# Three more ring slots and one more row group ahead in the second half of a sparse attention

## The chip, the cores and the metric

The kernel runs on one core of one Trainium2 chip. The metric is the device time of one execution in microseconds (us). Before the change the median of three runs was 1874.77 us (1874.08 to 1879.82).

A core has engines that run their own instruction streams side by side: TensorE (PE in the profile; PEld is its weight load), VectorE (DVE), ScalarE (ACT), GpSimd (POOL) and SyncE (SP), and 16 DMA engines that move data. An engine works its stream in order and waits on semaphores for the others.

## The reference

One layer of graph attention over 4096 nodes with 512 features and 8 heads, followed by a feed-forward part. The adjacency matrix is 4096 x 4096 and sparse: the mean row has some 17 ones.

```python
hs = layer_norm(x, ln1_scale, ln1_bias)
ht = layer_norm(h_target, ln1_scale, ln1_bias)
q = (ht @ Wq + bq).reshape(T, H, HD) / sqrt(HD)
k = (hs @ Wk + bk).reshape(S, H, HD)
v = (hs @ Wv + bv).reshape(S, H, HD)
logits = where(adj != 0, einsum('thd,shd->hts', q, k), -1e30)
ctx = einsum('hts,shd->thd', softmax(logits), v).reshape(T, D)
ht = layer_norm(ht + ctx @ Wo + bo, ln2_scale, ln2_bias)
out = layernorm(x + ht + gelu(ht @ W1) @ W2)
```

(The masks of the nodes are left out here; all nodes are valid.)

## The kernel before

Keys and values of all nodes are computed once and stored in HBM as rows of 1024 numbers (`kvd`: 512 of key, 512 of value). From the adjacency matrix the kernel makes, per target node, the list of its neighbours. The targets are sorted by their degree and cut into 32 tiles of 128 targets; a tile has a cap, the largest number of neighbours that it provides for. This is done in two parts, the first and the second 2048 targets, so that the attention on the first part can run while the lists of the second are still made.

The attention then works in row groups. A group is up to three neighbours of each of a tile's 128 targets: three gathers of GpSimd, each of which fetches 128 rows of `kvd` into one slot of a ring in SBUF. There are 603 gathers in 211 groups; groups 106 to 210 belong to the second part.

```python
NA, NBT = len(CAPS_A), len(CAPS_B)
S = 3
RING = 17
...
ring = kp.tile([P, RING, 2 * D], F32, name="kv")     # 17 slots of 128 x 1024 numbers
...
SG = [(i, j0, min(S, cap - j0)) for i, (_, cap) in enumerate(TILES)
      for j0 in range(0, cap, S)]
place = [0]
for _, _, n in SG:
    if place[-1] + n > RING:
        place[-1] = 0
    place.append(place[-1] + n)
...
def issue(k):
    if k >= len(SG):
        return
    i, j0, n = SG[k]
    if j0 == 0:
        prefetch(i + 2)                    # the list of a later tile
        if i not in tqs:
            fronts[i] = front(i)           # the query tile: gather, norm, projection
            step(fronts, i)
        ...
    kvs[k] = ring[:, place[k]:place[k] + n, :]
    for j in range(n):
        gather(kvs[k][:, j, :], kvd[0:N + 1, :], recs[i][:, E0 + j0 + j:E0 + j0 + j + 1])
```

A group's work: VectorE multiplies the key halves with the query (line 1169) and sums per head (line 1173), ScalarE takes the exponential (lines 1177 and 1187), VectorE weights two of the three value halves (line 1132), ScalarE the third, eight heads one by one (line 1152). In the second part VectorE adds two of them (line 1136). TensorE then transposes and adds up the value halves in PSUM (`cps`, line 1140). The weighting of a group comes after the product of the next one:

```python
for k in range(AHEAD + 1):                       # AHEAD = 4
    issue(k)
...
    kv, tq = kvs.pop(k), tqs[i]
    nc.vector.tensor_tensor(kv[:, :n, :D], kv[:, :n, :D], ..., ALU.mult)      # line 1169
    nc.vector.tensor_reduce(lg[:, :n, :], ..., AX.X, ALU.add)                 # line 1173
    ...
    if pend:
        values(*pend.pop())          # the group before: lines 1132, 1136, 1140
        issue(k + AHEAD)             # rows of the group four further on
    ...
```

At the end of a tile `finish` divides by the sums, projects and normalises (lines 1037 to 1097). Beside the attention runs a second stream, `feed`: the feed-forward part of the tiles that are done (lines 1277 and 1286 on TensorE), with a gather of x and a store of the result on GpSimd (lines 952 and 1254). All gathers and stores stand in the one queue of GpSimd, as do small power operations for the norms (line 674).

The lists have work space of their own: two buffers of 4 KB per partition (`a`), three of 1 KB (`sg`) and small ones (`dec`, `dif`, `rank`, `ranki`, `b16`). They are last used when the lists of the second part are sorted and written out.

```python
a = lp.tile([P, QW], I32, name="a", bufs=2)
sg = lp.tile([P, QW], U8, name="sg", bufs=3)
dec = lp.tile([P, 2, SEG, 8], U16, name="dec")
```

Of the kernel before, what the change touches and what calls it, by code (L numbers as in the profile page):

```python
# [8 lines left out]
F32 = mybir.dt.float32  # L9
I32 = mybir.dt.int32  # L10
U8 = mybir.dt.uint8
# [6 lines left out]
P = 128  # L18
# [348 lines left out]
BF16 = mybir.dt.bfloat16  # L367
U8 = mybir.dt.uint8
U16 = mybir.dt.uint16
# [74 lines left out]
def adj_resnorm_kernel(  # L444
# [34 lines left out]
    N, D = x.shape  # L479
# [9 lines left out]
    QW = N // NQ  # L489
# [4 lines left out]
    SEG = NQ * SQ  # L494
# [6 lines left out]
    NA, NBT = len(CAPS_A), len(CAPS_B)  # L501
    PARTS = ((0, len(CAPS_A)), (len(CAPS_A), len(CAPS_B)))
    S = 3
    RING = 17

    const = ctx.enter_context(tc.tile_pool(name="const", bufs=1))
    dram = ctx.enter_context(tc.tile_pool(name="dram", bufs=1, space=DRAM))
# [22 lines left out]
    with tc.tile_pool(name="keep", bufs=1) as keep:  # L530
# [17 lines left out]
        with ExitStack() as late:  # L548
            lp = late.enter_context(tc.tile_pool(name="lists", bufs=1))
            kp = late.enter_context(tc.tile_pool(name="kv", bufs=1))  # L550
# [9 lines left out]

            ring = kp.tile([P, RING, 2 * D], F32, name="kv")

            def xrows(n):
                return ring[:, 12 + n % 5, :].rearrange("p (j d) -> p j d", j=G)
# [27 lines left out]
            one_c = lp.tile([P, 1], F32, name="one_c")  # L594

            def list_constants():
                io = lp.tile([P, QW], I32, name="a", bufs=2)
                nc.gpsimd.iota(io[:, :SQ * WS], pattern=[[0, SQ], [2, WS]], base=1,
                               channel_multiplier=0)

                nc.vector.tensor_copy(lio, io[:, :WQ])
                io = lp.tile([P, QW], I32, name="a", bufs=2)
                nc.gpsimd.iota(io[:, :2 * SEG], pattern=[[1, 2], [QW, NQ], [2 * WS, SQ]], base=0,
                               channel_multiplier=0)
                nc.gpsimd.iota(io[:, 2 * SEG:2 * SEG + NB], pattern=[[1, NB]], base=0,
                               channel_multiplier=0)

                nc.vector.tensor_copy(segoff.rearrange("p b q s -> p (b q s)"), io[:, :2 * SEG])
                nc.vector.tensor_copy(bins, io[:, 2 * SEG:2 * SEG + NB])

                nc.gpsimd.memset(lower, -1.0)
                nc.gpsimd.affine_select(out=lower, in_=lower, compare_op=ALU.is_ge, fill=0.0,
                                        base=0, pattern=[[-1, P]], channel_multiplier=1)
                for R, (i0, n) in zip(Rs, PARTS):
# [80 lines left out]
            def quarter(i, h):  # L695
                if i < NA + FILL:
                    a = ring[:, (i * NQ + h) % DEEP, :].bitcast(I32)
                else:
                    a = lp.tile([P, QW], I32, name="a", bufs=2)
                nc.sync.dma_start(a, adj[i * P:(i + 1) * P, h * QW:(h + 1) * QW])  # L700
                return a

            def edges(i):

                part = 1 if i >= NA else 0
                rec = Rs[part][:, i - PARTS[part][0], :]
                cand = lp.tile([P, SEG, 8], U16, name="cand", bufs=2)
                for h in range(NQ):
                    n = i * NQ + h
                    while len(adjs) < min(n + 2, NT * NQ):  # L710
                        adjs.append(quarter(*divmod(len(adjs), NQ)))
                    a, adjs[n] = adjs[n], None

                    sg = lp.tile([P, QW], U8, name="sg", bufs=3)
                    nc.scalar.activation(sg, a, AF.Sign, accum_out=dpart[:, i, h:h + 1])  # L715
                    ahead = min(n + DEEP - 1, n + 3 + n // 2)
                    while len(adjs) < min(max(n + 3, min(ahead, (NA + FILL) * NQ)), NT * NQ):
                        adjs.append(quarter(*divmod(len(adjs), NQ)))
                    wd = sg.bitcast(U16)
                    nc.vector.tensor_tensor(wd, wd, lio, ALU.mult)  # L720
                    for s, (w0, w1) in enumerate(SEGS):
                        nc.vector.max(cand[:, h * SQ + s, :], wd[:, w0:w1])  # L722
                    if h == 1:
                        keep_rest()
                    if h % 2 and moms:
                        moments(moms.pop(0))
                    yield 2.0
                dec = lp.tile([P, 2, SEG, 8], U16, name="dec")
                nc.vector.tensor_single_scalar(dec[:, 0], cand, 255, op=ALU.bitwise_and)
                nc.vector.tensor_single_scalar(dec[:, 1], cand, 8, op=ALU.logical_shift_right)  # L730
                gid = lp.tile([P, 2 * SEG, 8], F32, name="gid")
                dec = dec.rearrange("p b s e -> p (b s) e")
                off = segoff.rearrange("p b q s -> p (b q s)")
                nc.vector.scalar_tensor_tensor(gid, dec, 0.0,
                                               off.unsqueeze(2).to_broadcast([P, 2 * SEG, 8]),
                                               op0=ALU.is_gt, op1=ALU.mult)
                nc.vector.tensor_add(gid, gid, dec)
                flat = gid.rearrange("p s e -> p (s e)")
                for r in range(RE // 8):
                    top = rec[:, E0 + r * 8:E0 + (r + 1) * 8]  # L740
# [53 lines left out]
            def sort(part):  # L794

                i0, n = PARTS[part]
                me = slice(i0, i0 + n)
                pool, R = lp, Rs[part]
                nc.vector.tensor_reduce(deg[:, me], dpart[:, me, :], AX.X, ALU.add)
                nc.vector.tensor_copy(R[:, :, DEG], deg[:, me])  # L800
                dif = pool.tile([P, n], F32, name="dif")
                nc.vector.scalar_tensor_tensor(dif, deg[:, me], float(RE), cnt[:, me], op0=ALU.min,
                                               op1=ALU.not_equal)
                nc.vector.tensor_reduce(bad[:, 1 + part:2 + part], dif, AX.X, ALU.max)
                nc.vector.tensor_scalar(dif, deg[:, me], 0.0, float(NB - 1), op0=ALU.max,
                                        op1=ALU.min)
                b16 = pool.tile([P, n], BF16, name="b16")
                nc.vector.tensor_scalar(b16, dif, -1.0, float(NB - 1), op0=ALU.mult, op1=ALU.add)
                if part:
                    oh = pool.tile([P, QW], I32, name="a", bufs=2).bitcast(BF16)  # L810
                else:
                    oh = wp.tile([P, NB * n], BF16, name="oh")
                oh = oh[:, :NB * n].rearrange("p (b i) -> p b i", b=NB)
                nc.vector.tensor_tensor(oh, b16.unsqueeze(1).to_broadcast([P, NB, n]),
                                        bins.unsqueeze(2).to_broadcast([P, NB, n]), ALU.is_equal)
                ohf = oh.rearrange("p b i -> p (b i)")
                pos = pool.tile([P, QW], I32, name="a", bufs=2).bitcast(F32)
                pos = pos[:, :NB * n].rearrange("p (b i) -> p b i", b=NB)
                posf = pos.rearrange("p b i -> p (b i)")
                w = NB * n // 2  # L820
# [12 lines left out]
                    nc.tensor.matmul(pa, lower, ohf[:, sl], start=True, stop=True)  # L833
                    nc.vector.tensor_add(posf[:, sl], pa, posf[:, sl])
                nc.vector.tensor_mul(pos, pos, oh)
                rank = pool.tile([P, n], F32, name="rank")
                nc.vector.tensor_reduce(rank, pos.rearrange("p b i -> p i b"), AX.X, ALU.add)
                ranki = pool.tile([P, n], I32, name="ranki")
                nc.vector.tensor_copy(ranki, rank)
                yield 10.0  # L840
                for i in range(n):
# [157 lines left out]
                  for j0 in range(0, cap, S)]  # L999
            kvs, rests, fronts = {}, {}, {}  # L1000
            place = [0]
            for _, _, n in SG:
                if place[-1] + n > RING:
                    place[-1] = 0
                place.append(place[-1] + n)

            def step(gens, i):

                if i in gens and next(gens[i], StopIteration) is StopIteration:
                    del gens[i]  # L1010

            def issue(k):

                if k >= len(SG):
                    return
                i, j0, n = SG[k]
                if j0 == 0:
                    prefetch(i + 2)
# [96 lines left out]
            def attention():  # L1115
# [35 lines left out]
                        v = kv[:, S - 1, D + hd * HD:D + (hd + 1) * HD]  # L1151
                        nc.scalar.mul(v, v, pa[:, hd:hd + 1])  # L1152

                for k in range(AHEAD + 1):
                    issue(k)
                yield 0.0
                k = 0
                for group in GROUPS:
# [3 lines left out]
                    for i in group:  # L1162
                        cps = ps.tile([P, KC, P], F32, name="cps", bufs=2)
                        while k < len(SG) and SG[k][0] == i:
                            _, j0, n = SG[k]
# [13 lines left out]
                            yield cost * n  # L1179
                            if pend:  # L1180
                                values(*pend.pop())
                                issue(k + AHEAD)
                            advance()
                            if j0 == 0:

# [165 lines left out]
            def prepare():  # L1351
# [6 lines left out]
                for R, (i0, n) in zip(Rs, PARTS):  # L1358
                    Rf = R.bitcast(F32)
                    nc.vector.tensor_copy(Rf[:, :, RST], rs[:, i0:i0 + n])  # L1360
                    nc.vector.tensor_copy(Rf[:, :, RST + 1], nm[:, i0:i0 + n])
                nm = lp.tile([P, QW], I32, name="a", bufs=2)
                nc.sync.dma_start(nm[:NT, :P], nodemask.rearrange("(c p) -> c p", p=P))
                nmf = nm.bitcast(F32)[:NT, P:2 * P]
                nc.vector.tensor_scalar(nmf, nm[:NT, :P], 1.0, None, op0=ALU.not_equal)
# [69 lines left out]
```

## Time and profile before

| | value |
|---|---|
| median time of three runs | 1874.77 us |
| span of the profiled execution | 1873.0 us |
| mean granted clock of TensorE | 0.963 |
| row gathers (line 952, `kv`) | 603, 690.1 us of GpSimd |
| idle time of GpSimd before them | 499.2 us |
| row products (line 1169) | 211, 352.5 us of VectorE |
| idle time of VectorE before them | 108.9 us, of it 97.8 us for gathers |
| transposes of values (line 1140) | 2008, 264.5 us of TensorE, idle before them 54.2 us |
| feed-forward (lines 1277 and 1286) | 3200 matmuls, 946.2 us of TensorE |

A busy share is an average over stages. A line of a group names the source line, the engine, what is written and read, how often, the busy time and the mean of one, and then how long the engine stood idle before these instructions and who released it. A line of waits has the engine and line that waited, the one waited for, the total, the number of times and the longest. A line of stretches has, for each stretch of the span, the busy time of PE, PEld, DVE, ACT and POOL, the granted clock of TensorE (1.00 is full), the busy share of the DMA engines and GB/s.

### The profile page before, as it was taken

What the parts mean: (1) busy time and instruction counts of PE and PEld (TensorE: products, weight loads), DVE (VectorE), ACT (ScalarE), POOL (GpSimd) and SP (SyncE); (2) the same over time, 40 slices, a digit from 0 to 9 for tenths busy, and PEclk for the clock granted to TensorE, in tenths of its full rate; (3) what the DMA queues carried; (4) which work ended last, traced back from release to release, by engine and by line L of the source; (5) the groups of instructions that cost most, each with busy time, mean ns of one, the idle gap of its engine ahead of it and who ended that gap; (6) DMA issues with size and microseconds to landing.
All of it is one profiled execution on the core that took longest, in us unless ns stands there. A gap on an engine that the chain in (4) does not pass through costs nothing. (4 is left out here: it accounts for less than half of the span.)

```text
span 1873.0 us, 22926 instructions
## 1 busy us (share of the span) xinstructions
PE 1699.6 (91%) x7030; PEld 1097.4 (59%) x7030; DVE 1430.0 (76%) x2595; ACT 1242.5 (66%) x3133; POOL 881.9 (47%) x804
## 2 busy tenths in 40 slices
PE   7989884698998989999999989999999999999996
PEld 3444332466655656766666656566666566666664
DVE  6999855989998838677878889889877778788400
ACT  5777634577886737776777767777777677777411
POOL 1000143744545474656666666656555545554101
PEclk9999977898999999999999989999999999999998
DMA  9999949978877556777778778767676767766000
GB/s 348 375 373 377 348 154 341 330 269 300 306 276 252 203 170 213 262 242 258 260 248 283 276 268 279 267 229 251 225 240 227 259 219 236 238 222 222 23 1 24
DMA packets 147757, 463.28 MB, mean 247 GB/s; under 512 B 24468, under 2 KB 29160, under 8 KB 147624
## 3 DMA queue, kind: packets, MB, share of 16 engines
q0 software_dynamic: 95696, 342.19, 53.9%
q1 hardware_dynamic: 44112, 96.44, 14.5%
q10 hardware_dynamic: 7816, 23.08, 3.2%
q8 instruction: 58, 0.95, 0.2%
q14 instruction: 75, 0.61, 0.1%
HBM read 430.76 MB, written 30.89 MB: 246 GB/s over the span
## 5 line engine op out<-in xcount | busy, mean ns | idle before, releaser
L952 POOL DMA_INDIRECT kv<-kvd,rec x603 | 690.1, 1144 | 499.2 <-PE cps L1140 232.9
L1277 PE MATMUL pf<-h2T,w 128*128 128x256 f32 (+1 forms) x2176 | 475.6, 371 | 1.2 <-ACT h2T L1097 1.2
L1286 PE MATMUL po<-w,gt 128*128 128x512 f32 x1024 | 470.6, 601 | 3.3 <-ACT gt L1280 3.3
L1169 DVE TENSOR_TENSOR kv<-kv,tq 128x1536 f32<-128x1536 f32 (+2 forms) x211 | 352.5, 1676 | 108.9 <-DMA kv<-kvd,rec 97.8
L1277 PEld LDWEIGHTS pf<-h2T,w 128*128 128x128 f32 x2176 | 391.6, 193 | 65.8 <-issue 19.8
L1152 ACT ACTIVATE kv<-kv,pa 128x64 f32<-128x64 f32 x1520 | 391.5, 336 | 3.6
L1173 DVE TENSOR_REDUCE lg<-kv 128x24 f32<-128x1536 f32 (+2 forms) x211 | 350.7, 1668 | 1.7 <-ACT pa L1149 0.2
L1140 PE MATMUL cps<-ident,kv 128*128 128x128 f32 x2008 | 264.5, 279 | 54.2 <-DVE kv L1132 40.3
L1140 PEld LDWEIGHTS cps<-ident,kv 128*128 128x128 f32 x2008 | 238.0, 144 | 128.9 <-issue 49.2
L1286 PEld LDWEIGHTS po<-w,gt 128*128 128x128 f32 x1024 | 188.6, 193 | 193.8 <-issue 189.4
L1132 DVE TENSOR_TENSOR kv<-kv,p 128x1024 f32<-128x1024 f32 (+1 forms) x211 | 249.5, 1189 | 53.5 <-ACT p L1177 53.5
L674 POOL TENSOR_TENSOR n_rs<-n_ve,mhalf 128x2 f32<-128x2 f32 (+2 forms) x51 | 47.1, 924 | 335.2 <-DVE n_ve L667 150.9
L1280 ACT ACT_TABLE_LOAD x110 | 141.1, 1283 | 1.7
L917 PE MATMUL pq<-wk,h2T 128*128 128x512 f32 x256 | 125.3, 634 | 15.8 <-ACT h2T L902 8.1
L722 DVE MAX8 cand<-sg 128x8 uint16<-128x103 uint16 (+1 forms) x640 | 131.9, 251 | 0.5
L991 PE MATMUL t<-wq,tq 128*128 128x512 f32 x256 | 118.5, 606 | 10.8 <-ACT tq L985 8.0
L715 ACT ACTIVATE sg<-kv 128x1024 uint8<-128x1024 int32 x84 | 88.7, 1058 | 56.8 <-DMA kv<-in_adj_dram 23.4
L1280 ACT ACTIVATE gt<-pf 128x512 f32<-128x512 f32 x128 | 76.4, 597 | 75.0 <-PE pf L1277 73.9
L1067 PE MATMUL t<-wo,rb 128*128 128x512 f32 x256 | 119.2, 610 | 3.6 <-DVE rb L1057 3.6
L917 PE MATMUL pq<-wv,h2T 128*128 128x512 f32 x256 | 116.7, 598 | 1.3 <-ACT tq L919 1.3
L917 PEld LDWEIGHTS pq<-wk,h2T 128*128 128x128 f32 x256 | 49.8, 202 | 81.9 <-issue 51.4
L1177 ACT ACT_TABLE_LOAD x67 | 86.0, 1283 | 9.2 <-DVE lg L1173 7.4
(157 smaller groups left out, 1544.4 us busy)
## 6 DMA issues: line engine op xcount, KB each, us to landing
kv<-in_adj_dram SPq DMA_DIRECT2D x84, 512.0 KB, 7.5
a<-in_adj_dram SPq DMA_DIRECT2D x44, 512.0 KB, 6.4
kvd<-tq ACTq DMA_DIRECT2D x24, 512.0 KB, 6.6
kv<-kvd,rec POOLq DMA_INDIRECT x603, 5.7
kv<-in_L_gnn_h_target_dram SPq DMA_DIRECT2D x32, 256.0 KB, 7.7
kv<-in_x_dram SPq DMA_DIRECT2D x15, 512.0 KB, 8.9
rest_d<-gid SPq DMA_DIRECT2D x32, 160.0 KB, 5.0
w<-in_L_gnn_W_dram SPq DMA_DIRECT2D x4, 1024.0 KB, 9.5
```

What stands on the lines that cost most here:

```text
L722: nc.vector.max(cand[:, h * SQ + s, :], wd[:, w0:w1])
L917: nc.tensor.matmul(pkv, hT[:, kc, j * P:(j + 1) * P], w[:, kc, :], start=kc == 0, stop=kc == KC - 1)
L952: nc.gpsimd.indirect_dma_start(out=dst, out_offset=None, in_=table[:, :], in_offset=bass.IndirectOffsetOnAxis(ap=idx, axis=0))
L1067: nc.tensor.matmul(pa, ct[:, c, :], wo[:, c, :], start=False, stop=c == KC - 1, skip_group_check=True)
L1132: nc.vector.tensor_tensor(v4, v4, p[:, j0:j0 + m, :].unsqueeze(3) .to_broadcast([P, m, H, HD]), ALU.mult)
L1140: nc.tensor.matmul(cps[:, c, :], kv[:, j, D + c * P:D + (c + 1) * P], ident, is_transpose=True, start=j0 + j == 0 and c == 0, stop=j0 + n ...
L1152: nc.scalar.mul(v, v, pa[:, hd:hd + 1])
L1169: nc.vector.tensor_tensor(kv[:, :n, :D], kv[:, :n, :D], tq[:, :D].unsqueeze(1).to_broadcast([P, n, D]), ALU.mult)
L1173: nc.vector.tensor_reduce(lg[:, :n, :], kv[:, :n, :D].rearrange("p j (h d) -> p j h d", h=H), AX.X, ALU.add)
L1277: nc.tensor.matmul(pf[:, k, :], w1[(f0 + k) // KC][:, kc, (f0 + k) % KC * P:((f0 + k) % KC + 1) * P], h2T[:, kc, :w], start=kc == 0, stop= ...
L1280: nc.scalar.activation(gt, pf, AF.Gelu_apprx_tanh)
L1286: nc.tensor.matmul(po[j], gt[:, k, j * P:(j + 1) * P], w2[(f0 + k) // KC][:, (f0 + k) % KC, :], start=False, stop=f0 + k == FC - 1, skip_g ...
```

## The change

From the second part on, the ring has 20 slots in place of 17, and the rows are requested five groups ahead in place of four. The room for the three slots comes from the lists: their work buffers are no longer allocated for themselves but lie in slots 17 to 19, which the first part of the attention doesn't use and which are free when the second part needs them. It is meant to give the row gathers of the second part more time before their rows are needed.

```diff
-    RING = 17
+    RING = (17, 20)
...
-            ring = kp.tile([P, RING, 2 * D], F32, name="kv")
+            ring = kp.tile([P, RING[1], 2 * D], F32, name="kv")
+            wide = [ring[:, 17 + i, :].bitcast(I32) for i in range(2)]
+            tools = ring[:, 19, :]
+            signs = [tools[:, i * QW // 4:(i + 1) * QW // 4].bitcast(U8) for i in range(3)]
+            dec_w = tools[:, 768:768 + SEG * 8].bitcast(U16).rearrange(...)
...
-                    a = lp.tile([P, QW], I32, name="a", bufs=2)
+                    a = turn_of("wide", wide)          # so at all six places of "a"
...
-                    sg = lp.tile([P, QW], U8, name="sg", bufs=3)
+                    sg = turn_of("signs", signs)
...
-                dif = pool.tile([P, n], F32, name="dif")
+                dif, rank = tools[:, 928:928 + n], tools[:, 944:944 + n]
+                ranki, b16 = tools[:, 960:960 + n].bitcast(I32), tools[:, 976:984].bitcast(BF16)
...
-            for _, _, n in SG:
-                if place[-1] + n > RING:
+            for i, _, n in SG:
+                if place[-1] + n > RING[i >= NA]:
                     place[-1] = 0
                 place.append(place[-1] + n)
+            first_b = next(k for k, (i, _, _) in enumerate(SG) if i >= NA)
...
+            def request(k):
+                ahead = AHEAD + (1 if k >= first_b else 0)
+                while issued[0] <= min(k + ahead, len(SG) - 1):
+                    issue(issued[0])
+                    ...
+                    issued[0] += 1
...
-                for k in range(AHEAD + 1):
-                    issue(k)
+                request(0)
...
                                 values(*pend.pop())
-                                issue(k + AHEAD)
+                                request(k)
```

More of the change, by code (lines that the diff above doesn't have):

```diff
@@ L559, in adj_resnorm_kernel, with turn_of @@
             psi = mid.enter_context(tc.tile_pool(name="psi", bufs=1, space=PSUM))
-            ring = kp.tile([P, RING, 2 * D], F32, name="kv")
+            ring = kp.tile([P, RING[1], 2 * D], F32, name="kv")
+            wide = [ring[:, 17 + i, :].bitcast(I32) for i in range(2)]
+            tools = ring[:, 19, :]
+            signs = [tools[:, i * QW // 4:(i + 1) * QW // 4].bitcast(U8) for i in range(3)]
+            dec_w = tools[:, 768:768 + SEG * 8].bitcast(U16).rearrange("p (b s e) -> p b s e",
+                                                                       b=2, s=SEG)
+            turns = {"wide": 0, "signs": 0}
+            def turn_of(name, places):
+                turns[name] += 1
+                return places[turns[name] % len(places)]
             def xrows(n):
@@ L596, in list_constants @@
             def list_constants():
-                io = lp.tile([P, QW], I32, name="a", bufs=2)
+                io = turn_of("wide", wide)
                 nc.gpsimd.iota(io[:, :SQ * WS], pattern=[[0, SQ], [2, WS]], base=1,
@@ L601, in list_constants @@
                 nc.vector.tensor_copy(lio, io[:, :WQ])
-                io = lp.tile([P, QW], I32, name="a", bufs=2)
+                io = turn_of("wide", wide)
                 nc.gpsimd.iota(io[:, :2 * SEG], pattern=[[1, 2], [QW, NQ], [2 * WS, SQ]], base=0,
@@ L727, in edges @@
                     yield 2.0
-                dec = lp.tile([P, 2, SEG, 8], U16, name="dec")
+                dec = dec_w
                 nc.vector.tensor_single_scalar(dec[:, 0], cand, 255, op=ALU.bitwise_and)
@@ L806, in sort @@
                                         op1=ALU.min)
-                b16 = pool.tile([P, n], BF16, name="b16")
                 nc.vector.tensor_scalar(b16, dif, -1.0, float(NB - 1), op0=ALU.mult, op1=ALU.add)
                 if part:
-                    oh = pool.tile([P, QW], I32, name="a", bufs=2).bitcast(BF16)
+                    oh = turn_of("wide", wide).bitcast(BF16)
                 else:
@@ L816, in sort @@
                 ohf = oh.rearrange("p b i -> p (b i)")
-                pos = pool.tile([P, QW], I32, name="a", bufs=2).bitcast(F32)
+                pos = turn_of("wide", wide).bitcast(F32)
                 pos = pos[:, :NB * n].rearrange("p (b i) -> p b i", b=NB)
@@ L835, in sort @@
                 nc.vector.tensor_mul(pos, pos, oh)
-                rank = pool.tile([P, n], F32, name="rank")
                 nc.vector.tensor_reduce(rank, pos.rearrange("p b i -> p i b"), AX.X, ALU.add)
-                ranki = pool.tile([P, n], I32, name="ranki")
                 nc.vector.tensor_copy(ranki, rank)
@@ L1001, in adj_resnorm_kernel @@
             place = [0]
-            for _, _, n in SG:
-                if place[-1] + n > RING:
+            for i, _, n in SG:
+                if place[-1] + n > RING[i >= NA]:
                     place[-1] = 0
                 place.append(place[-1] + n)
+            first_b = next(k for k, (i, _, _) in enumerate(SG) if i >= NA)
+            issued = [0]
             def step(gens, i):
@@ L1010, in step @@
                     del gens[i]
+            def request(k):
+                ahead = AHEAD + (1 if k >= first_b else 0)
+                while issued[0] <= min(k + ahead, len(SG) - 1):
+                    issue(issued[0])
+                    mine = set(range(place[issued[0]], place[issued[0]] + SG[issued[0]][2]))
+                    for m in range(k, issued[0]):
+                        assert not mine & set(range(place[m], place[m] + SG[m][2]))
+                    issued[0] += 1
             def issue(k):
-                if k >= len(SG):
-                    return
                 i, j0, n = SG[k]
@@ L1361, in prepare @@
                     nc.vector.tensor_copy(Rf[:, :, RST + 1], nm[:, i0:i0 + n])
-                nm = lp.tile([P, QW], I32, name="a", bufs=2)
+                nm = turn_of("wide", wide)
                 nc.sync.dma_start(nm[:NT, :P], nodemask.rearrange("(c p) -> c p", p=P))
```

## The prediction

> **What bounds the kernel now.** I read the page first: the busy shares, then the stretches of the second part of the attention, then the waits in it by engine, last the order of time around single waits.
>
> ```profile
> PE 1699.6 (91%) x7030; PEld 1097.4 (59%) x7030; DVE 1430.0 (76%) x2595; ACT 1242.5 (66%) x3133; POOL 881.9 (47%) x804
> ```
>
> TensorE is busy for 91% of the span, so it is the engine whose gaps are worth anything. The chain of waits of the page covers only the last 17 us and tells nothing of the part that the change touches; I left it. The change acts from group 106 of 211 on (the first row group of tile 16). In the trace its product (line 1169) starts at 1042.3 us and the last one, of group 210, at 1733.6 us. So I cut the span there, with columns of busy us per engine, the granted clock and the share of the DMA engines:
>
> ```profile
> 1040.00:1220.00 180.00, 164.09 (x701) 111.70 (x700) 157.21 (x160) 132.03 (x364) 119.46 (x102) 0.93 0.79 266
> 1220.00:1740.00 520.00, 502.67 (x2128) 334.50 (x2127) 418.37 (x446) 380.96 (x989) 283.28 (x255) 0.99 0.70 231
> 1740.00:1873.00 133.00, 114.31 (x488) 76.56 (x486) 15.83 (x77) 27.34 (x55) 11.28 (x13) 0.95 0.05 17
> ```
>
> TensorE idles 180 - 164.1 = 15.9 us in the first stretch and 520 - 502.7 = 17.3 us in the second: 33 us in all. That is the whole stock of idle time that a change to the second part can take away, 1.8% of the span. The clock tells a second, smaller stock: 0.93 in the first stretch. Now who waits for whom between 1040 and 1740 us (total, times, longest):
>
> ```profile
> POOL kv L952 <- PE cps L1140: 77.8, 52, 6.4
> POOL kv L952 <- DVE kv L1136: 76.3, 36, 5.8
> ...
> DVE kv L1169 <- DMA kv<-kvd,rec: 37.2, 20, 6.8
> ...
> PE cps L1140 <- DVE kv L1136: 13.9, 6, 5.0
> ```
>
> GpSimd stands for 154 us before row gathers, because the ring slot they write is still being read (77.8 + 76.3). VectorE stands for 37.2 us because rows have not landed. TensorE stands for only 13.9 us behind the value half of the ring (line 1136, after which the transposes of line 1140 run). This falling series, 154, 37, 14, is the point: most of the wait is slack and only its end reaches the bound. The rest of TensorE's 33 us are waits for ScalarE in the front and finish of a tile (line 982 6.0, 1063 5.1, 991 4.0, 1093 3.4 us, summed from its gaps), which no ring slot cures.
>
> How one such gap comes about, in order of time (start, length, engine, line; idle before it in brackets), GpSimd first, then VectorE, then TensorE:
>
> ```profile
> 1181.78 2.54 POOL L1254 DMA_INDIRECT out_dram<-xt,rec  x1 [0.30 <-ACT kv L1152]
> 1187.35 0.97 POOL L952 DMA_INDIRECT xt<-in_x_dram,rec  x1 [3.02 <-DMA out_dram<-xt,rec]
> ...
> 1202.37 1.76 DVE L1169 TENSOR_TENSOR kv<-kv,tq 128x1536 f32<-128x1536 f32 x1 [4.43 <-DMA kv<-kvd,rec]
> ...
> 1200.45 3.60 PE L1067 MATMUL t<-wo,rb 128*128 128x512 f32 x8
> 1207.58 1.97 PE L1140 MATMUL cps<-ident,kv 128*128 128x128 f32 x8 [3.53 <-DVE kv L1136]
> ```
>
> GpSimd is held by a store and by a gather of x, the row gathers of group 133 go out late (1189.9 to 1196.7 us), VectorE's product for them starts 4.43 us late, the weighting of the group before stands behind it on VectorE, and TensorE loses 3.53 us. The half clock follows; the same view of the four short stretches after the cps gaps:
>
> ```profile
> 1056.50:1059.90 3.40, 3.34 (x12) 3.07 (x13) 1.23 (x2) 3.40 (x13) 2.79 (x3) 0.50 0.96 284
> 1090.60:1097.40 6.80, 3.84 (x11) 2.77 (x12) 6.80 (x7) 6.53 (x18) 4.09 (x4) 0.50 0.85 282
> ...
> 1135.00:1138.40 3.40, 3.40 (x6) 1.34 (x5) 3.40 (x3) 1.67 (x2) 2.39 (x2) 0.50 0.98 236
> 1206.70:1213.50 6.80, 5.92 (x13) 3.45 (x14) 5.75 (x8) 3.74 (x15) 3.39 (x4) 0.50 0.78 249
> ```
>
> **What the Trainium skill says.** "Perfetto Trace Analysis", Optimization Strategy: a gap that keeps repeating on the engine that should be full can mean too little SBUF for the next tile. The 154 us of GpSimd agree in kind; but the gap is on GpSimd, not on the full engine, which is why I count little of it. "TensorE: Matmul & The Clock Gate", What's actually happening: the array falls to half clock after an idle window of about 3.4 us and needs about as long of work to come back. The trace agrees: stretches of 3.4 and 6.8 us at 0.50 beside gaps of 2.15 to 5.00 us. The same page, Architectural detail, says that GpSimd works its queue strictly in order; the trace agrees (1187.35 us above: the gathers wait behind the store's landing). "DMA: Bandwidth & Descriptors", Rules for kernel authors: issue a DMA early and wait for it late. A gather here takes 5.5 us from issue to landing (median, 4.1 to 7.4), and from the end of a group's last gather to its use I find 11.5 us in the median, but under 6.2 us in 11 of the 105 groups, 7 of them among the first 28. Those few are what is to be gained.
>
> **The change, part by part.**
>
> *Work.* No gather, product or matmul is added or removed: 603 gathers, 211 groups. Only where the rows lie and when they are asked for changes.
>
> *List work space in the ring.* The same number of buffers (two wide, three sign), now parts of slots 17 to 19. In the built program the order on every engine, and nearly every wait, is that of before until the end of the first part, since rows there still use 17 slots and four groups ahead. I expect nothing before some 1000 us: 0 us. The lists' last use of that space is the 16 scatters of the second part's records, the last from 676.8 us; the first row group of the second part is gathered from 1028.9 us, some 350 us later, so nobody waits for the three slots.
>
> *Three more slots.* With 17 slots, a group of the second part overwrites the slot of the group 5 or 6 before it (59 and 42 groups); with 20, of the one 6 or 7 before it (54 and 46). Each request also stands one group earlier in the program. Tied together: a gather waits for the same event as before, but is for the next group. A group lasts (1733.6 - 1042.3) / 104 = 6.6 us, so the time between landing and use grows by some 6.6 us where GpSimd is waiting for a slot. Leads of 4.4 to 6.2 become 11 to 13 us against 5.5 us of landing. The waits of VectorE for rows should fall from 37.2 us to 5 to 10.
>
> *What of this reaches TensorE.* The cps gaps, 13.9 us. Then the half clock behind them: work done at half clock takes twice its time, so half of its busy time is lost: (3.34 + 3.84 + 3.40 + 5.92) / 2 = 8.3 us. Together 22.2 us.
>
> *What I take off.* In the built program row gathers stand 3 to 5 gathers earlier against the other GpSimd instructions nearly everywhere, but around the pair of stores and x gathers near gather 380 they stand where they did. That is the gap at 1207 us, 3.5 us and 3.0 us of clock, which I leave: 15.7 us remain. Of those I count four fifths, because once VectorE has its rows it runs into other waits (28.5 us for the probabilities of ScalarE, 37.4 us for the query product): 12.6 us.
>
> *End.* After 1740 us only the feed-forward part is left, 114 us of TensorE work in 133 us. It is unchanged and starts earlier by what was saved.
>
> Sum: 1874.8 - 12.6 = 1862, which I round to 1861, as earlier requests may shave some of the front waits too.
>
> **Rivals.** (1) *Hidden anyway.* VectorE's lateness is taken up by the other stream on TensorE, and the gaps move to the ScalarE waits: saving 0 to 5 us, 1870 to 1875. For it: VectorE's two other large waits in this stretch, 28.5 and 37.4 us, have nothing to do with rows. Against: of the four largest gaps of TensorE in the second part (5.00, 3.53, 3.34, 2.86 us) three stand directly before cps. (2) *All of it.* Every row wait goes, the clock stays up and the fronts, which start a group earlier, lose their waits too: 33 us plus some 13 us of half clock (seven stretches, 26.4 us busy) give a floor of 1829. Against: fronts and finishes keep their distances in program order. (3) *A new wait.* More rows in flight fill the DMA queues (0.79 busy already in the first stretch), or GpSimd blocks in its queue for a query tile not yet free, or the scheduler's new local order hurts ScalarE: 5 to 15 us lost, 1880 to 1890. Against: bytes are the same, and the wait of query gathers for the finish (line 1063) is 0.3 us here.
>
> **Range and chances.** The middle is 1861. Below, rival 2 in half reaches 1848; above, rival 1 ends at 1875. I take 1848 to 1875. Faster by over 2% means under 1837, which needs over 37 of at most 46 us: 0.05. Slower by over 2% means over 1912; nothing in the change costs that: 0.02.
>
> **What would show it.** Right: in the first 1000 us the two profiles agree; from there the waits of VectorE for rows fall below 12 us, the wait of cps for line 1136 below 5 us, and the half-clock stretches between 1050 and 1220 us go from five to one or two. GpSimd's waits for slots stay near 150 us, as the ring is full again, one group further on. Wrong: VectorE's row waits vanish and TensorE's idle time in the second part stays near 33 us (rival 1), or gaps before lines 982, 991 and 1063 grow. A difference before 1000 us would mean that the shared work space costs waits that I did not see.

## The result, and the profile after

The changed kernel takes 1882.36 us (median of four runs, 1879.70 to 1885.35). The kernel before, run beside it, takes 1876.01 us. The ratio is 1.0032 with a 95% interval of 1.0007 to 1.0056. I had expected 1861 us, in a range of 1848 to 1875: the change costs 0.3% where I expected it to bring 0.7%.

The page of the changed kernel shows the same busy TensorE in a slightly longer span:

```profile
PE 1698.0 (90%) x7030; PEld 1097.0 (58%) x7030; DVE 1429.2 (76%) x2595; ACT 1233.1 (66%) x3127; POOL 887.3 (47%) x804
```

The second part, cut at the same times as in the prediction (busy us of PE, PEld, DVE, ACT and POOL, granted clock, share of the DMA engines, GB/s):

```profile
1040.00:1220.00 180.00, 167.68 (x731) 114.11 (x730) 163.74 (x166) 136.96 (x387) 121.44 (x106) 0.97 0.82 281
1220.00:1740.00 520.00, 488.00 (x2052) 324.83 (x2051) 408.70 (x439) 365.16 (x956) 279.46 (x246) 0.98 0.66 222
```

The two halves of the second part go opposite ways. In the first stretch TensorE idles 180 - 167.7 = 12.3 us, where it idled 15.9, and its clock is 0.97 for 0.93: a gain. In the second it idles 520 - 488 = 32.0 us, where it idled 17.3, and its clock is 0.98 for 0.99: a loss. If each matmul is set against the matmul of the same number in the trace before, the changed kernel is 7 us ahead when the second part begins (TensorE's order of instructions is the same up to there, so I take this for scatter), 16 us ahead at 1290 us and 4 us behind at the end. About 9 us were won up to 1290 us, and 20 us lost after it.

The waits of the same 700 us (engine and line that waited, released by; total, times, longest). The lines of the changed kernel are numbered some 20 higher: 1157 is the addition that was 1136, 1161 the transposes of values that were 1140, 1189 the product that was 1169; 992, 995 and 1001 are the front's transposes, its copies by ScalarE and its query matmul; 1084 and 1092 are the finish's transposes and its copy of h.

```profile
POOL kv L962 <- DVE kv L1157: 77.9, 36, 7.1
...
POOL kv L962 <- PE cps L1161: 59.1, 31, 5.9
...
DVE kv L1189 <- DMA kv<-kvd,rec: 22.3, 13, 6.3
...
PE t L1084 <- ACT tq L995: 11.1, 2, 7.3
...
PE t L992 <- ACT h L1092: 8.7, 2, 5.9
...
PE cps L1161 <- DVE kv L1157: 5.8, 2, 4.2
```

VectorE's wait for rows fell from 37.2 to 22.3 us, and TensorE's wait for the value half from 13.9 to 5.8 us. In the place of these stand two waits of TensorE for ScalarE, 11.1 and 8.7 us; the same pairs were 3.0 and 3.6 us before:

```profile
PE t L982 <- ACT h L1071: 3.6, 2, 3.3
PE t L1063 <- ACT tq L985: 3.0, 2, 1.6
```

All waits of TensorE for ScalarE in this stretch sum to 37.1 us; before, to 16.6.

How the largest gap comes about, in order of time (start, length, engine, line; idle before it in brackets):

```profile
1466.07 0.60 PE L992 MATMUL t<-ident,tq 128*128 128x128 f32 x4
...
1467.38 2.74 PE L1306 MATMUL po<-w,gt 128*128 128x512 f32 x6
...
1468.47 2.02 ACT L1173 ACTIVATE kv<-kv,pa 128x64 f32<-128x64 f32 x8
...
1470.86 1.22 DVE L1189 TENSOR_TENSOR kv<-kv,tq 128x1024 f32<-128x1024 f32 x1 [1.30 <-DMA kv<-kvd,rec]
...
1472.61 1.21 DVE L1193 TENSOR_REDUCE lg<-kv 128x16 f32<-128x1024 f32 x1
...
1473.85 0.19 ACT L1197 ACTIVATE p<-lg 128x16 f32<-128x16 f32 x1 [3.37 <-DVE lg L1193]
1474.06 1.28 ACT L1300 ACT_TABLE_LOAD   x1
1475.35 0.60 ACT L1300 ACTIVATE gt<-pf 128x512 f32<-128x512 f32 x1
1475.84 1.50 ACT L995 ACTIVATE tq<-t,b1r,cols 128x128 f32<-128x128 f32 x4
1477.39 1.12 PE L1084 MATMUL t<-ident,tq 128*128 128x128 f32 x4 [7.28 <-ACT tq L995]
```

TensorE writes the front's transposes into the PSUM tile `t` at 1466.1 us. The next user of `t` is the finish (line 1084), and it needs the front's copies (line 995) done. They are 1.5 us of work, but in ScalarE's list they stand behind a third value half of 2.02 us, an exponential that waits 3.37 us for VectorE's logits, and a GELU with its table load. They start at 1475.8 us, over 9 us after the transposes, and end at 1477.3 us, 10.7 us after them. In that time TensorE has only some 3.5 us of other work (its last, line 1306, ends at 1470.1 us), so it stands for 7.28 us.

Half clock comes with the new gaps as it came with the old ones:

```profile
1054.00:1057.40 3.40, 3.13 (x14) 3.04 (x15) 2.04 (x3) 1.77 (x8) 2.48 (x4) 0.50 0.88 298
1108.60:1115.40 6.80, 6.01 (x18) 4.90 (x19) 6.80 (x7) 4.44 (x13) 1.19 (x2) 0.50 0.76 270
...
1381.70:1388.50 6.80, 3.28 (x10) 2.84 (x11) 6.35 (x14) 5.36 (x15) 3.62 (x5) 0.50 0.41 125
1473.80:1480.60 6.80, 3.21 (x7) 1.93 (x8) 4.62 (x9) 3.46 (x7) 3.51 (x5) 0.50 0.95 353
```

The last two stretches begin 2.4 and 3.7 us after their gap began, while TensorE still stands, so half of each holds no matmul (3.28 and 3.21 us of 6.80 are busy). The four transposes at 1477.39 us take 1.12 us at half clock, those at 1466.07 us 0.60 us at full clock.

Between 1050 and 1220 us 10.2 us of half clock are left. But there are 20.4 us of it between 1290 and 1573 us, and the sum over the second part is 30.6 us in both kernels.

### The profile page after: what moved, and what is told of

The parts are those of the page before. It is cut to its first block, busy times and chain, and to the rows that moved or that the text cites. A ratio compares the mean times of both kernels' runs of the same rounds, so it can differ in the third digit from the quotient of the medians.

```text
span 1877.7 us, 22906 instructions
## 1 busy us (share of the span) xinstructions
PE 1698.0 (90%) x7030; PEld 1097.0 (58%) x7030; DVE 1429.2 (76%) x2595; ACT 1233.1 (66%) x3127; POOL 887.3 (47%) x804
## 3 DMA queue, kind: packets, MB, share of 16 engines
q1 hardware_dynamic: 44112, 96.44, 14.3%
## 5 line engine op out<-in xcount | busy, mean ns | idle before, releaser
L1306 PE MATMUL po<-w,gt 128*128 128x512 f32 x1024 | 464.1, 593 | 2.1 <-issue 1.6
L1161 PEld LDWEIGHTS cps<-ident,kv 128*128 128x128 f32 x2008 | 237.6, 144 | 108.5 <-issue 54.4
L1153 DVE TENSOR_TENSOR kv<-kv,p 128x1024 f32<-128x1024 f32 (+1 forms) x211 | 249.9, 1191 | 51.2 <-ACT p L1197 41.2
L727 ACT ACTIVATE kv<-kv 128x1024 uint8<-128x1024 int32 x128 | 134.9, 1055 | 90.1 <-DMA kv<-in_adj_dram 45.6
L734 DVE MAX8 cand<-kv 128x8 uint16<-128x103 uint16 (+1 forms) x640 | 132.5, 253 | 0.5
L1197 ACT ACTIVATE p<-lg 128x24 f32<-128x24 f32 (+2 forms) x179 | 33.7, 188 | 106.8 <-DVE lg L1193 80.2
```

Source lines behind the costliest of these rows:

```text
L1153: nc.vector.tensor_tensor(v4, v4, p[:, j0:j0 + m, :].unsqueeze(3) .to_broadcast([P, m, H, HD]), ALU.mult)
L1161: nc.tensor.matmul(cps[:, c, :], kv[:, j, D + c * P:D + (c + 1) * P], ident, is_transpose=True, start=j0 + j == 0 and c == 0, stop=j0 + n ...
L1306: nc.tensor.matmul(po[j], gt[:, k, j * P:(j + 1) * P], w2[(f0 + k) // KC][:, (f0 + k) % KC, :], start=False, stop=f0 + k == FC - 1, skip_g ...
```

## The experiments

What had I not counted? `issue` does two things at a tile's first group: it asks for rows, and it begins the tile's front (gather of the target rows, norm, transposes, copies, query matmul). Asking five groups ahead in place of four moves both. **Theory A**: the rows gain, and the front, one group earlier, loses more. **Theory B**: more rows in flight lose. **Theory C**: the shared work space costs.

All times are medians; the ratio is to the kernel before, run beside it. Idle is TensorE's from 1040 to 1740 us, half clock the time at 0.50 in about the same stretch, "for ScalarE" the sum of TensorE's waits for ScalarE and "rows" VectorE's wait for rows from 1040 to 1740 us.

| kernel | slots | rows ahead | front ahead | us | ratio (95% interval) | idle | half clock | for ScalarE | rows |
|---|---|---|---|---|---|---|---|---|---|
| before | 17 | 4 | 4 | 1876.01 | | 33.2 | 30.6 | 16.6 | 37.2 |
| changed | 20 | 5 | 5 | 1882.36 | 1.0032 (1.0007 to 1.0056) | 44.3 | 30.6 | 37.1 | 22.3 |
| e4 | 17 | 4 | 4 | 1877.03 | 1.0000 (0.9983 to 1.0017) | 40.9 | 20.4 | 20.3 | 39.8 |
| e1 | 20 | 4 | 4 | 1857.71 | 0.9886 (0.9862 to 0.9910) | 26.7 | 10.2 | 14.3 | 12.1 |
| e3 | 20 | 5 | 4 | 1853.30 | 0.9877 (0.9853 to 0.9901) | 22.5 | 13.6 | 13.3 | 10.4 |
| e5 | 17 | 4 | 5 | 1902.71 | 1.0153 (1.0128 to 1.0178) | 53.5 | 47.8 | 41.2 | 70.2 |
| e7 | 20 | 5 | gather 5, rest about 4 | 1851.13 | 0.9856 (0.9836 to 0.9877) | 18.4 | 10.2 | 6.5 | 10.3 |
| e6 | 20 | 5 | 3 | 1858.53 | 0.9914 (0.9894 to 0.9934) | 21.8 | 17.0 | 3.6 | none |
| e10 | 20 | 5 | 5, own bank | 1871.51 | 0.9971 (0.9960 to 0.9981) | 35.8 | 30.6 | 25.1 | 28.7 |
| e11 | 20 | 5 | 4, own bank | 1867.39 | 0.9947 (0.9928 to 0.9966) | 29.8 | 34.0 | 18.9 | 14.9 |
| e12 | 20 | 5 | 5 | 1873.42 | 1.0001 (0.9984 to 1.0018) | 39.9 | 17.0 | 32.1 | 25.8 |
| e13 | 20 | 5 | 4 | 1860.75 | 0.9939 (0.9917 to 0.9962) | 28.9 | 20.4 | 18.8 | 13.0 |

(From e10 on the probabilities lie in SBUF from tile 20 on; see there.)

The idle time and half of the matmul time at half clock carry most of these differences (the column counts idle time too, which must not be counted twice): the changed kernel has 44.3 - 22.5 = 21.8 us more idle time than e3 and, with 22.4 us of matmuls in its half clock stretches against 11.6, 5.4 us more lost to the clock. That is 27 us, where the two profiled spans are 1877.7 - 1851.1 = 26.6 us apart.

**e4: the shared work space alone.** 17 slots and four groups ahead, with the lists' buffers in the ring.

```diff
-                if place[-1] + n > RING[i >= NA]:
+                if place[-1] + n > 17:
...
-                ahead = AHEAD + (1 if k >= first_b else 0)
+                ahead = AHEAD
```

> Only the work space of the lists moves into the ring's last three slots; 17 slots and four groups ahead everywhere. Instruction order is that of before on every engine. Theory A and B: as before, ratio 1.000 within 0.002. Theory C: the 6 us of the changed kernel, 1881 to 1884 us.

1877.03 us, ratio 1.0000. Theory C falls; the work space in the ring costs nothing that can be measured.

**e1: the three slots alone.** The changed kernel with rows and front four groups ahead, as before.

```diff
-                ahead = AHEAD + (1 if k >= first_b else 0)
+                ahead = AHEAD
```

> 20 slots in the second part, but rows and query tiles requested four groups ahead as before. Theory A (the query front of a tile, which the longer request starts one group earlier, loses what the rows gain): the rows still get their slots one group earlier, the front stands where it was, so 1855 to 1866 us. Theory B (more rows in flight lose by themselves: the query gathers, the x gathers and the stores wait behind them): slower than before, 1880 to 1885 us. Theory C (the shared work space costs): 1880 us or more.

1857.71 us: 1.1% faster than before, with nothing left of the change but the slots and the shared work space that makes room for them. A gather now writes the slot of a group that lies one further back; GpSimd's waits for slots fall from 154 to 134 us, and VectorE's wait for rows to 12.1 us.

**e3: rows five groups ahead, front four.** `issue` is split in two; the front begins in a loop of its own, `begin` (the list request stays with it, and so does the request of the rest list, which holds those neighbours of a large tile that its list has no room for), and `issue` asks for rows alone.

```diff
+                front_ahead = AHEAD + ((0) if k >= first_b else 0)
+                while begun[0] <= min(k + front_ahead, last):
+                    begin(begun[0])
...
                 while issued[0] <= min(k + ahead, last):
                     issue(issued[0])
```

> The changed kernel, but only the rows are requested five groups ahead; the query front, the list request and the rest list of a tile start four groups ahead as before. Theory A: the 20 us that the changed kernel loses between 1290 and 1590 us stay away, 1855 to 1866 us, and the waits of TensorE before the finish's transposes (11.1 us in the changed kernel) fall below 5 us. Theory B: as the changed kernel, 1880 to 1885 us. Theory C: as the changed kernel.

1853.30 us, a little under the range of Theory A: this version beats both kernels, and Theory B falls, since as many rows are in flight here as in the changed kernel. From e1 it can't be told apart: the slots bring the gain, the earlier request adds nothing measurable. VectorE's and TensorE's waits in e3 (its lines are numbered differently again: 1201 is the product, 1173 the transposes of values):

```profile
DVE kv L1201 <- DMA kv<-kvd,rec: 10.4, 3, 7.8
```

```profile
PE cps L1173 <- DVE kv L1169: 7.0, 4, 4.2
PE t L1001 <- ACT tq L995: 5.0, 3, 3.2
...
PE t L1126 <- ACT h L1117: 3.9, 1, 3.9
```

The waits of the finish for the front's copies, 11.1 us in the changed kernel (line 1084), and of the front for the copy of h, 8.7 us, are gone as large gaps: none of the waits for ScalarE is longer than 3.9 us.

**e5: the front alone one group earlier.** 17 slots and rows four groups ahead as before, with `front_ahead = AHEAD + 1` in the second part.

```diff
-                if place[-1] + n > RING[i >= NA]:
+                if place[-1] + n > 17:
...
+                front_ahead = AHEAD + ((1) if k >= first_b else 0)
+                ahead = AHEAD
```

> 17 slots and rows four groups ahead as before (with the work space in the ring), but the query front and the list request of a tile start five groups ahead in the second part. Theory A: the loss without the gain, 1885 to 1895 us, with waits of TensorE for ScalarE before the front's and the finish's transposes of over 15 us in the second part. Theory B: as before, 1874 to 1880 us.

1902.71 us, 8 us beyond the range of Theory A and 25.7 us above e4, from which it differs only in the place of the front and of the list requests that begin with it. So the loss needs neither the slots nor the rows. Its waits show that the loss spreads to everything behind it:

```profile
POOL kv L962 <- DVE kv L1169: 98.1, 38, 7.6
...
DVE kv L1201 <- DMA kv<-kvd,rec: 70.2, 33, 6.6
```

VectorE waits 70.2 us for rows, and GpSimd 98.1 us for the addition that frees a slot; e4 has 39.8 and 77.8 us. In this kernel a row wait may thus come from a front that stands badly; how it delays VectorE and GpSimd stays open.

**e7: which part of the front?** The changed kernel, with two empty steps after the front's gather in the second part. The gather stays five groups ahead; norm, transposes, copies and query matmul come about where they stood before the change.

```diff
                 gather(t, h_target, rec[:, TGT:TGT + 1])
                 yield
+                if i > NA:
+                    yield
+                    yield
                 m = rec[:, RST:RST + 2].bitcast(F32)
```

> The changed kernel, but in the second part the front's steps after its gather begin two steps later, so that its transposes, copies and query matmul stand about where they stood before the change, while the gather of the target rows stays five groups ahead. Theory A (the early transposes and copies lose): 1852 to 1862 us. Rival (the early gather loses, as it holds one of three query tiles longer and makes GpSimd wait for it): 1875 to 1885 us.

1851.13 us, just under the range of Theory A: two empty steps in the program turn a loss of 0.3% into a gain of 1.4%. So the early gather, the query tile that is held longer and the early list requests cost nothing; the early computing does. TensorE's waits here (line 1164 is the transposes of values, 1004 the query matmul, 998 the front's copies, 1095 the copy of h):

```profile
PE cps L1164 <- DVE kv L1160: 7.8, 5, 4.1
PE t L1004 <- ACT tq L998: 1.9, 2, 1.6
PE t L1004 <- ACT h L1095: 1.8, 1, 1.8
```

Copies come late here too. In order of time (line 995 is the front's transposes):

```profile
1381.38 0.60 PE L995 MATMUL t<-ident,tq 128*128 128x128 f32 x4
...
1386.12 3.62 PE L1300 MATMUL pf<-h2T,w 128*128 128x256 f32 x16
1389.77 1.50 ACT L998 ACTIVATE tq<-t,b1r,cols 128x128 f32<-128x128 f32 x4
1391.33 3.70 PE L1004 MATMUL t<-wq,tq 128*128 128x512 f32 x8 [1.58 <-ACT tq L998]
```

They end 9.3 us after their transposes, against 10.7 us at the gap of 7.28 us in the changed kernel. But here the finish does not come between, TensorE has 7.8 us of other work before the query matmul needs them, and it stands for 1.58 us only. (This is an earlier tile than the one of the gap.)

**e6: later still.** e3 with `front_ahead = AHEAD - 1` in the second part.

> 20 slots, rows five groups ahead, front three groups ahead: one group later still than e3. If every group of lateness moves the front to a better place: 1840 to 1850 us. If four groups is about the best distance and the query product now comes late for VectorE (its wait for the query tile, 37.4 us in the kernel before, grows): 1855 to 1870 us. I expect the second, about 1858.

1858.53 us, as expected. TensorE waits only 3.6 us for ScalarE, but 14.9 us for the value half, and VectorE 54.4 us for the query product (41.6 in e3), so the front now comes late for the tile that it serves. Of the three distances tried, that of the kernel before is the best, but the 5 us between e6 and e3 are no more than a mere reordering moves in the runs below.

**e10 to e13: is it the bank?** Front and finish take turns in one PSUM bank, `t`. The Trainium skill, "Perfetto Trace Analysis", Matmuls, advises to rotate independent groups of matmuls through different banks, so that the evacuation of one lies beside the next. The gap at 1477 us looks like a case of that. e10 is the changed kernel and e11 is e3, both with the front's two PSUM tiles in the bank of the probabilities from tile 22 on, for which the probabilities move to SBUF from tile 20 on (into a buffer of the lists that is free by then):

```diff
-                pt = ps.tile([P, KC, P], F32, name="t")
+                pt = ps.tile([P, KC, P], F32, name="t" if i < 22 else "p")
...
-                pq = ps.tile([P, D], F32, name="t")
+                pq = ps.tile([P, D], F32, name="t" if i < 22 else "p")
...
-                                p = ps.tile([P, MAXE, H], F32, name="p")
+                                if i < 20:
+                                    p = ps.tile([P, MAXE, H], F32, name="p")
+                                else:
+                                    p = lp.tile([P, 2 * SEG, 8], F32, name="gid").rearrange(...)
```

> The changed kernel (20 slots, rows and front five groups ahead) with one thing altered from tile 22 on: the front's transposes and its query matmul use a PSUM bank of their own, so they no longer take turns with the finish in the bank t (the probabilities move from that bank to SBUF from tile 20 on). Theory A1 (the early front loses because it takes turns with the finish in one bank): 1850 to 1862 us, no more than 6 us above the same with a late front (e11); the gaps of TensorE before the transposes of the product of the finish behind an evacuation of the front, 7.28 us at 1477 us, and before the transposes of the front behind the copy of h, 5.94 us at 1385 us, are gone. Theory A2 (it loses because ScalarE works in order and the front's copies stand at worse places of its list): 1875 to 1885 us, 20 us or more above e11.

> The kernel of e3 (20 slots, rows five groups ahead, front four) with the front in a bank of its own from tile 22 on, as in e10. Both theories: 1845 to 1855 us, at or a little under the 1853.3 of e3, since waits for that bank are few there.

e10 takes 1871.51 us and e11 1867.39 us. Both theories missed e11, which lies 14 us above e3, and e10 falls between their two ranges, though the two gaps that Theory A1 names are gone and e10 lies within 6 us of e11, as it expects. So I ran the other half of the edit by itself, the probabilities in SBUF with the front in `t`: e12 on the changed kernel, e13 on e3.

> The changed kernel with only the other half of e10: the probabilities lie in SBUF from tile 20 on, the front stays in the bank t. If the place of the probabilities costs by itself (up to the 14 us that e11 lies above e3): 1885 to 1897 us, and then the own bank of e10 is worth 15 to 25 us with an early front. If it costs nothing: 1880 to 1885 us, and the own bank is worth some 11 us.

> The kernel of e3 with only the probabilities moved to SBUF from tile 20 on, the front in the bank t. If the place of the probabilities is what made e11 14 us longer than e3: 1862 to 1870 us. If it is the front's bank (the query matmul in the bank that tile 20 still reads, or its place in the order): 1851 to 1857 us.

e12 takes 1873.42 us, 9 us less than the changed kernel, against both expectations; e13 takes 1860.75 us, 7 us more than e3, just under the first of its two ranges. Moving the probabilities thus makes one kernel faster and the other slower. The edit also reorders the lists of ScalarE and VectorE, and that may be what moves the time, by 7 to 9 us in either direction. The bank is therefore read from pairs that differ in little else, and from their ratios, as the two of a pair were timed at different times, each beside the kernel before. With the early front, e10 against e12, these are 0.9971 and 1.0001: 0.3% for the bank of its own. With the late front, e11 against e13, they are 0.9947 and 0.9939: nothing (by the medians e11 is 6.6 us longer). The early front costs 0.6% in the shared bank (e12 against e13) and 0.2% with the bank of its own (e10 against e11). That would make sharing part of the loss, but 0.3% is no more than the move of the probabilities does by itself (1.0032 to 1.0001, 0.9877 to 0.9939), so what the bank is worth is not shown. What changes for certain is which matmuls wait. In e12:

```profile
PE t L992 <- ACT h L1092: 7.0, 2, 4.9
...
PE t L1084 <- ACT tq L995: 5.6, 2, 5.3
PE t L1001 <- ACT tq L995: 5.4, 3, 3.1
```

In e10, with the bank of its own:

```profile
PE p L1001 <- ACT tq L995: 14.1, 4, 4.3
```

The transposes of the finish (line 1084) and of the front (line 992) no longer wait for ScalarE, and the query matmul waits for the same copies, 14.1 us in place of 5.4: it needs them whatever the bank. One of the four, in order of time:

```profile
1384.91 0.60 PE L992 MATMUL p<-ident,tq 128*128 128x128 f32 x4
...
1386.77 0.81 ACT L988 ACTIVATE tq<-tq,rec 128x512 f32<-128x512 f32 x1 [2.71 <-DMA tq<-in_L_gnn_h_target_dram,rec]
...
1387.95 2.02 ACT L1173 ACTIVATE kv<-kv,pa 128x64 f32<-128x64 f32 x8
...
1390.67 0.62 ACT L1068 COPY rb<-ri 128x512 f32<-128x512 f32 x1 [0.70 <-DVE ri L1065]
1391.19 1.51 ACT L1105 ACTIVATE h<-h,n_nm,n_rs 128x512 f32<-128x512 f32 x2
1392.62 1.48 ACT L995 ACTIVATE tq<-p,b1r,cols 128x128 f32<-128x128 f32 x4
...
1394.14 3.12 PE L1001 MATMUL p<-wq,tq 128*128 128x512 f32 x4 [4.31 <-ACT tq L995]
```

The copies start 7.1 us after their transposes. They stand behind the norm of the next query tile, for whose gather ScalarE waits 2.71 us, behind a third value half, a copy of the finish and its norm of h. The Trainium skill, "TensorE: Matmul & The Clock Gate", Architectural detail, calls ScalarE's queue strictly first in, first out; both timelines agree (1.5 us of copies start 9 and 7 us after their transposes). That the place in ScalarE's list alone makes the loss does not follow. Over the 15 fronts between 1040 and 1740 us the copies end 4.6 us after their transposes in the mean in the changed kernel, 4.1 us in e3 and 4.0 us in e7, while TensorE's waits for them sum to 16.9, 6.6 and 2.8 us. So how soon TensorE needs the tile or the copies counts as well, and the early front moves that too. e3, e5 and e7 move both at once, and no run separates them. No version was run with the copies on another engine.

## Why the prediction was wrong

- **List work space in the ring, 0 us:** right. e4 has the ratio 1.0000.
- **Three more slots:** right in kind. VectorE's wait for rows was to fall from 37.2 to 5 to 10 us; it falls to 10.4 us in e3 and 12.1 us in e1. In the changed kernel it is 22.3 us; the early front by itself raises it (e5 by 30 us over e4). In the second part, 11 groups had under 6.2 us between the end of their last gather on GpSimd and their use; in the changed kernel 2 have. But "each request also stands one group earlier" isn't needed: e1 without it gains as much.
- **What of this reaches TensorE, and what I take off:** too small. I counted 12.6 us; with the front's computing in its old place the slots bring 1.1% to 1.4% (18.6 us in e1, 23.0 in e3, 25.5 in e7 between the medians). In e3 the idle time falls by 33.2 - 22.5 = 10.7 us, of which the value half has 13.9 - 7.0 = 6.9, where I counted four fifths of 10.4, or 8.3. Matmul time at half clock falls from 26.4 to 11.6 us, half of which is 7.4, where I counted four fifths of 5.3, or 4.2. So the value half brings less than I counted, and the clock and the waits for ScalarE (16.6 us before, 13.3 in e3) bring more. I had left out three of the seven stretches of half clock (at 1118, 1254 and 1483 us, 10.2 of 30.6 us), as they follow no gap before the value half but waits for ScalarE, which I took for fixed; in e3 there is none after 1217 us.
- **The step that failed** stands in rival 2: "fronts and finishes keep their distances in program order". They don't. The front begins with the first row group of its tile, which is asked for five groups ahead; the finish begins with the last group of its tile, which the change doesn't move. So the front moves one group against the finish, the exponentials and everything else in the lists of ScalarE and TensorE. The part-by-part sum, which began with "Only where the rows lie and when they are asked for changes", therefore had no term for it. The term measures 25.7 us (e5 against e4), 29 us (the changed kernel against e3), 31 us (against e7) and 12.7 us where the lists are ordered otherwise (e12 against e13).
- **Rival 3** named the outcome, 1880 to 1890 us, and that is in part luck: it counted 5 to 15 us of loss, and 1882 us is a gain of 23 us (e3) less a loss of 29. Of its three causes, the new order that hurts ScalarE is in keeping with the timelines, though they show TensorE's order as much. The other two were not it: the DMA queues (e3 has as many rows in flight) and a query tile not yet free (e7). I gave it little weight because I considered the order of the row gathers alone.
- **What would show it:** of the two signs of being wrong, "gaps before lines 982, 991 and 1063 grow" came true for two: from 6.0 to 11.6 us for the first (now line 992) and from 5.1 to 12.5 us for the last (now 1084); the query matmul's went from 4.0 to 3.4. Of the signs of being right, the half clock stretches between 1050 and 1220 us did go from five to two, but the waits for rows (22.3 us) and for the value half (5.8 us) stayed above the 12 and 5 us named. GpSimd's waits for slots, expected to stay near 150 us, are 137.0 us.

## What to carry to other kernels

A request function that serves several streams moves all of them when its distance grows: list what else hangs on it, and split it, before counting what the longer distance brings. Here buffers alone brought 1.1%, and one group of distance on a second stream took it all back.

Where two streams share engines that work through lists, a late copy costs the full engine only what its other work doesn't cover: 10.7 us against 3.5 us of work cost 7.3 us and a stretch of half clock, 9.3 us against 7.8 us cost 1.6. So look both at what the releasing engine did before, and at what the waiting engine has to do until then, and try a later place as well as an earlier one. A buffer of its own for the victim is no sure cure: here the wait went to the next instruction that needs the same copies.

## What was not expected of the hardware

With the probabilities moved from PSUM to SBUF the changed kernel takes 1873.42 in place of 1882.36 us, and e3 takes 1860.75 in place of 1853.30: opposite signs for the same edit (by the ratios 0.3% less and 0.6% more). The order of instructions on ScalarE, VectorE and GpSimd moves with it, which I take for the reason, but no run separates it. In this kernel differences of some 10 us between two builds whose lists are ordered otherwise say little about the edit itself. The 6 us between the kernel before and the changed one are of that size too; what carries the verdict is that the early front loses 25.7, 29 and 31 us in the three pairs with the probabilities in PSUM, well above that size. With them in SBUF it loses 12.7 us with the shared bank and 4 us with its own, which is little or no more than that size. And part of the cost of a gap lies behind it, as much as there is work in the half clock: 3.0 us behind the gap of 3.53 us at 1207 us in the kernel before (half of 5.92), but only 1.6 us each behind the gaps of 5.94 and 7.28 us at 1385 and 1477 us in the changed one, where TensorE stood for half of the stretch.
